# Gates of the spatial layers: the root in halves, pooling by block, and moves issued from two queues

## The chip, the cores and the metric

The program runs on one core of a Trainium2 chip. A core has TensorE (matrix products, written PE; its weight loads PEld), VectorE (DVE), ScalarE (ACT), GpSimd (POOL) and SyncE (SP), each with its own in-order stream of instructions, and 16 DMA engines that move data between and within the memories when an engine issues a transfer. The metric is the device time of one execution in microseconds; less is better. Engines order themselves by semaphores, which the framework places from the reads and writes of tiles.

## The reference

Four layers run on x, eight images of 64 channels and 64 by 64 pixels: a selective scan with a gate behind it, a spatial and channel attention, a modifier with inner gradient steps, and one more attention. The change lies in the gate at the end of the first layer:

```python
def _channel_ln(x, g, b):
    u = jnp.mean(x, 1, keepdims=True)
    v = jnp.mean((x - u) ** 2, 1, keepdims=True)
    return (x - u) * jax.lax.rsqrt(v + CN_EPS) * g[None, :, None, None] + b[None, :, None, None]
...
def _safm(x, mfr_w, mfr_b, aggr_w, aggr_b):
    parts = jnp.split(x, 4, axis=1)
    outs = []
    for i in range(4):
        s = parts[i]
        k = 2 ** i
        if i > 0:
            s = jax.lax.reduce_window(s, -jnp.inf, jax.lax.max, (1, 1, k, k), (1, 1, k, k), 'VALID')
        s = _dwconv3(s, mfr_w[i], mfr_b[i])
        if i > 0:
            s = jnp.repeat(jnp.repeat(s, k, axis=2), k, axis=3)
        outs.append(s)
    out = jnp.concatenate(outs, axis=1)
    out = jnp.einsum('bchw,oc->bohw', out, aggr_w) + aggr_b[None, :, None, None]
    return jax.nn.gelu(out, approximate=False) * x
...
xo = jnp.transpose(xh, (0, 3, 1, 2))
return xo + _safm(_channel_ln(xo, cn_g, cn_b), mfr_w, mfr_b, aggr_w, aggr_b)
```

So each pixel is normalised over its 64 channels; the channels are split into four parts of 16, part i is pooled by maximum over 2^i by 2^i pixels, convolved 3 by 3 channel by channel, brought back to full size, mixed by a 64 by 64 matrix, put through gelu, multiplied with the normalised image, and added to the image.

## The kernel before

`gate_and_attention` works on the images in pairs: the 128 partitions hold 2 images of 64 channels, the free dimension the 4096 pixels. For each of the four pairs (`for p in range(NB // 2)`) it loads x, normalises, gates, and then runs the next layer's attention on it. All of the pair's gate stands on the way to its attention: nothing of another pair lies beside it except the last products of the attention before. "Pair 0" to "pair 3" below are these four.

**Normalisation** (`Common.pair_norm`, L128 to L163). The image is cut into 4 blocks of 1024 pixels (16 image rows). For each block a product with a centring matrix subtracts the mean (L137, tile cps), VectorE copies the result into the interior of the padded image pad0 (L140), ScalarE squares it (L142), and a product with `avg` (L145) puts the variance of 512 pixels into two rows of `var`. One [16, 512] tile thus holds the variance of all pixels. Its root is taken in three steps over 16 partitions: add eps (L150, VectorE), Sqrt (L151, ScalarE), Reciprocal (L152, VectorE). Then for each block a product with `spread`, which has 16 rows, copies the two roots that belong to the block to all channels (L157, tile rps), VectorE multiplies (L162) and ScalarE applies gain and bias (Identity, L163).

**Pooling** (L1473, L1475). When all four blocks are normalised, VectorE takes the maximum over columns and then over rows, for the whole image, three times; the results go to the padded images pad1 (32 by 32), pad2 (16 by 16), pad3 (8 by 8).

**Moves** (`move`, L1423). The convolution is a product over 48 rows per image: 16 channels times three vertical shifts. A tile "mv" holds these, and each is filled by six transfers within SBUF, of 16 partitions each: two images (e) times three shifts (dy). There are tiles for pad3 (1), pad2 (1), pad1 (2) and pad0 (3 tiles for 4 blocks, so that block 3 reuses block 0's), so a pair has 8 moves and 48 transfers. SP issues all of them. Its order in the built program is: three transfers of pad0's first move, both moves of pad1 (12), pad2 (6), pad3 (6), and then the rest of pad0 (21).

**Convolutions** (`conv`, L1433, tile cvps). They run from the smallest image up: pad3, pad2, two of pad1, and four blocks of pad0, each with its result doubled and added to the next (`doubled` L1445, `add_doubled` L1454). A product of 512 columns leaves two records of TensorE in the trace. For each block of pad0 follow gelu on ScalarE (L1504), the product with the normalised image (L1505) and the sum into x (L1506) on POOL.

PSUM comes from three pools: "sc" with three buffers (cps, rps, cvps and the attention's scores), "av" with one (var), and "mm" with one (the attention's small products fps, qps and sumps, and in the setup the transposes tps and bps of the weights). A tile of a pool with one buffer waits until the one before it has been read. The setup of the gate's and the attention's weights (`safm_setup`, `Attention.__init__`; L1060 to L1119 in the trace) is issued ahead of pair 0 and runs beside its normalisation. The framework schedules the instructions of each engine from their order in the program and from when they can run; transfers take eight semaphores in turn, and a transfer waits until the one before it on its semaphore has landed.

Of the kernel before, what the change touches and what calls it, by code (L numbers as in the profile page):

```python
# [10 lines left out]
F32 = mybir.dt.float32  # L11
BF16 = mybir.dt.bfloat16
AF = mybir.ActivationFunctionType
ALU = mybir.AluOpType
# [5 lines left out]
C = 64  # L20
S = 64
L = S * S
BK = 512
NBK = L // BK
# [20 lines left out]
class Common:  # L45
# [60 lines left out]
    def pair_norm_consts(self):  # L106

        nc = self.nc  # L110
        cen = self.tile([2 * C, 2 * C], "p_cen")
        nc.vector.memset(cen, 0.0)
        avg = self.tile([2 * C, 4 * NBK - 2], "p_avg")
        nc.vector.memset(avg, 0.0)
        for e in range(2):
            rows, m = slice(e * C, (e + 1) * C), 2 * NBK - 2 + e
            nc.vector.tensor_scalar(
                cen[rows, rows], self.ident[rows, rows], -1.0 / C, None, ALU.add
            )
            nc.vector.memset(avg[rows, m : m + 1], 1.0 / C)  # L120
        spread = self.tile([2 * NBK, 2 * NBK, C], "p_spread")
        nc.vector.tensor_copy(
            spread,
            self.ident[: 2 * NBK, : 2 * NBK].unsqueeze(2).to_broadcast([2 * NBK, 2 * NBK, C]),
        )
        return cen, avg, spread

    def pair_norm(self, work, sc, var, src, dst, consts, eps, g, b):  # L128

        nc = self.nc
        cen, avg, spread = consts
        for i in range(NBK // 2):
            ps = sc.tile([128, 2, BK], F32, name="cps", tag="sc")
            for e in range(2):
                nc.tensor.matmul(  # L137
                    ps[:, e, :], cen, src[:, bass.ts(2 * i + e, BK)], start=True, stop=True
                )
            nc.vector.tensor_copy(dst(i), ps.rearrange("p e (r c) -> p (e r) c", c=S))  # L140
            sq = work.tile([128, 2, BK], F32, name="sq", tag="blk", bufs=3)
            nc.scalar.activation(sq, ps, AF.Square)  # L142
            for e in range(2):
                m = 2 * (NBK - 1 - 2 * i - e)
                nc.tensor.matmul(  # L145
                    var[: 2 * NBK], avg[:, m : m + 2 * NBK], sq[:, e, :],
                    start=(i + e == 0), stop=(2 * i + e == NBK - 1),
                )
        rstd = work.tile([2 * NBK, BK], F32, name="rstd", tag="rstd", bufs=1)
        nc.vector.tensor_scalar(rstd, var[: 2 * NBK], eps, None, ALU.add)  # L150
        nc.scalar.activation(rstd, rstd, AF.Sqrt)  # L151
        nc.vector.reciprocal(rstd, rstd)  # L152
        for i in range(NBK // 2):
            ps = sc.tile([128, 2, BK], F32, name="rps", tag="sc")
            for e in range(2):
                j = 2 * (2 * i + e)
                nc.tensor.matmul(  # L157
                    ps[:, e, :], spread[:, j : j + 2, :].rearrange("k e c -> k (e c)"), rstd,
                    start=True, stop=True,
                )  # L160
            out = dst(i)
            nc.vector.tensor_tensor(out, out, ps.rearrange("p e (r c) -> p (e r) c", c=S), ALU.mult)  # L162
            nc.scalar.activation(out, out, AF.Identity, bias=b, scale=g)  # L163


class Background:
# [1208 lines left out]
def gate_and_attention(cm, xh, w, a, x1, mixes, x2):  # L1375


    tc, nc = cm.tc, cm.nc
    halves = [slice(e * C, (e + 1) * C) for e in range(2)]
    with ExitStack() as ctx:  # L1380
# [17 lines left out]
        pads = []  # L1398
        for i in range(4):
            n = S // 2**i + 2  # L1400
# [15 lines left out]
        rows = BK // S  # L1416
        q = C // 4

        def move(i, r0, t):

            for e in range(2):
                for dy in range(3):
                    nc.sync.dma_start(  # L1423
                        t[e * C + dy * q : e * C + (dy + 1) * q],
                        pads[i][e * C + i * q : e * C + (i + 1) * q,
                                r0 + dy : r0 + dy + t.shape[1], :],
                    )
# [32 lines left out]
        for p in range(NB // 2):  # L1460
            x = io.tile([2 * C, L], F32, name="x", tag="x")
# [2 lines left out]
            def inner(i):  # L1464
                return pads[0][:, 1 + 2 * i * rows : 1 + 2 * (i + 1) * rows, 1 : S + 1]

            var = avp.tile([128, BK], F32, name="var", tag="av")
            cm.pair_norm(work, sc, var, x, inner, cn, 1e-6, cn_g, cn_b)
            src = pads[0][:, 1 : S + 1, 1 : S + 1]
            for i in range(1, 4):  # L1470
                n = S // 2**i
                m = one.tile([2 * C, 2 * n, n], F32, name=f"max{i}", tag=f"wide{n}")
                nc.vector.tensor_tensor(m, src[:, :, 0::2], src[:, :, 1::2], ALU.max)  # L1473
                src = pads[i][:, 1 : n + 1, 1 : n + 1]
                nc.vector.tensor_tensor(src, m[:, 0::2, :], m[:, 1::2, :], ALU.max)  # L1475
                for r, t in enumerate(moved[i]):
                    move(i, part * r, t)
            p3 = bank(8, 8)
            conv(p3, 3, moved[3][0], 0, 8)
            d3 = doubled(p3, 8, 8)  # L1480
# [33 lines left out]
            for j in range(TQ // 8):  # L1514
                ps = sc.tile([128, 8, 2 * C], F32, name="xTps", tag="sc")
# [674 lines left out]
```

## Time and profile before

Three runs before: median 12229.28 us (12226.62 to 12230.54). The profiled execution took 12228.28 us, its span is 12226.5 us.

| | |
|---|---|
| span of the profiled execution | 12226.5 us |
| busy PE, DVE, ACT, POOL | 11196.6, 10380.4, 7575.7, 7247.3 us |
| the gates: pair 0, from x's issue to x1's issue | 6949.67 to 7060.54 us |
| pair 1, from its first product L137 to x1's issue | 7483.41 to 7577.25 us |
| pair 2 | 7996.81 to 8091.79 us |
| pair 3 | 8514.51 to 8608.30 us |
| transfers of the moves | 192, all issued by SP |

The gates take some 395 us of the span. A row of a timeline gives start, duration, engine, line, operation, result and operands, and in brackets the idle time of the engine ahead of it and what ended it. In stretches, PEclk is the clock that TensorE was granted, as a share of the full one.

### The profile page before, as it was taken

How to read it: one execution, taken by the hardware profiler on the slowest of the kernel's cores; microseconds unless marked ns; L12 is line 12 of the kernel's file. 1: busy time of each engine (PE TensorE's matmuls, PEld its weight loads, DVE VectorE, ACT ScalarE, POOL GpSimd, SP SyncE). 2: the span in 40 equal slices, each digit the busy share in tenths (PEclk: the TensorE clock that was granted, in tenths of full speed). 3: DMA queues.
4: the chain of work that ended last, by engine and by line, in shares of the span. 5: the costliest groups of instructions: out<-in, count | busy, mean ns of one | idle time of the engine just before them, and what ended most of it. 6: DMA issues, size and time to landing. Idle time of an engine off the chain costs nothing. (4 is left out here: it accounts for less than half of the span.)

```text
span 12226.5 us, 120204 instructions
## 1 busy us (share of the span) xinstructions
PE 11196.6 (92%) x39087; PEld 4103.2 (34%) x39087; DVE 10380.4 (85%) x7400; ACT 7575.7 (62%) x10304; POOL 7247.3 (59%) x3326
## 2 busy tenths in 40 slices
PE   7899999999999999999998799999987779999999
PEld 2233333333333333333322233232335463333333
DVE  4999999999999999999999776868778676676767
ACT  4666667766667676676675554645547574555554
POOL 4999999999999999999999500000007480000000
PEclk8999999999999999999999899999998779999999
DMA  3666666666666666666666400000011100000000
GB/s 112 205 210 217 210 211 214 212 212 210 213 212 207 210 216 209 212 213 211 205 203 211 135 20 25 6 25 8 17 49 34 41 20 24 19 4 19 5 11 6
DMA packets 522899, 1528.62 MB, mean 125 GB/s; under 512 B 125312, under 2 KB 142352, under 8 KB 519696
## 3 DMA queue, kind: packets, MB, share of 16 engines
q1 hardware_dynamic: 522256, 1520.80, 37.9%
q8 instruction: 312, 5.11, 0.2%
q14 instruction: 331, 2.71, 0.1%
HBM read 1439.63 MB, written 72.09 MB: 124 GB/s over the span
## 5 line engine op out<-in xcount | busy, mean ns | idle before, releaser
L816 POOL TENSOR_TENSOR ct<-ct,h 128x1024 f32<-128x1024 f32 x2048 | 4789.4, 2362 | 296.8 <-DVE h L811 133.1
L882 PE MATMUL yps<-ct,lno_cen 128*128 128x512 f32 x8192 | 4119.9, 633 | 58.6 <-ACT yps L869 57.2
L811 DVE TENSOR_TENSOR_SCAN h<-a,state,z 128x1024 f32<-128x1024 f32 x1536 | 3570.4, 2341 | 82.5 <-ACT z L777 39.7
L762 ACT ACTIVATE a<-dt,amat 128x1024 f32<-128x1024 f32 x2048 | 2347.1, 1147 | 1134.8 <-DVE h L811 1128.1
L1191 DVE TENSOR_TENSOR sum<-sum,ex 128x1024 f32<-128x1024 f32 x1920 | 2347.5, 1223 | 618.5 <-ACT ex L1184 483.1
L1184 ACT ACTIVATE ex<-sc 128x1024 f32<-128x1024 f32 x2048 | 1968.0, 1024 | 1359.6 <-PE sc L1179 1359.2
L882 PEld LDWEIGHTS yps<-ct,lno_cen 128*128 128x128 f32 x8192 | 1476.4, 195 | 2078.9 <-issue 1818.0
L807 DVE TENSOR_TENSOR z<-z,e 128x1024 f32<-128x1024 f32 x1536 | 1859.8, 1211 | 128.0 <-PE z L780 75.5
L1198 PE MATMUL av<-ex,v 128*64 128x512 f32 x8192 | 1950.0, 604 | 0.0
L1179 PE MATMUL sc<-q,k 16*128 16x512 f32 (+1 forms) x8192 | 1562.1, 623 | 4.2 <-ACT q L1172 3.1
L780 PE MATMUL z<-bs,pick 48*128 48x512 bf16 x3072 | 941.9, 387 | 388.4 <-DVE h L811 339.5
L811 DVE TENSOR_TENSOR_SCAN h<-a,z 128x1024 f32<-128x1024 f32 x512 | 1161.3, 2281 | 75.0 <-ACT z L777 59.8
L770 POOL TENSOR_TENSOR bt<-bt,e 128x1024 f32<-128x1024 f32 x512 | 1209.8, 2363 | 5.4 <-DMA bt<-bc 5.4
L1505 POOL TENSOR_TENSOR gt<-gt,pad 128x1024 f32<-128x1024 f32 x16 | 34.9, 2179 | 1575.0 <-ACT gt L1504 1575.0
L1198 PEld LDWEIGHTS av<-ex,v 128*64 128x64 f32 x8192 | 512.2, 136 | 1332.7 <-issue 1278.9
L1179 PEld LDWEIGHTS sc<-q,k 16*128 16x128 f32 (+1 forms) x8192 | 528.2, 184 | 1016.4 <-issue 977.4
L777 ACT COPY z<-bt 128x1024 f32<-128x1024 f32 x512 | 519.9, 1015 | 406.0 <-DVE h L811 309.2
L780 PEld LDWEIGHTS <-pick 48*128 48x128 bf16 x3072 | 175.9, 95 | 1514.5 <-DVE h L811 931.4
L534 PE MATMUL vps<-pad,convd 128*128 128x512 f32 x1152 | 573.8, 599 | 0.1
L1878 DVE RECIPROCAL r<-e 128x512 f32<-128x512 f32 x128 | 420.6, 3322 | 0.0
L1881 POOL TENSOR_TENSOR r<-r,half 128x512 f32<-128x512 f32 x128 | 162.7, 1271 | 361.9 <-issue 186.0
L798 ACT COPY state<-h 128x1 f32<-128x1 f32 x2048 | 362.9, 177 | 0.0
(417 smaller groups left out, 9594.8 us busy)
## 6 DMA issues: line engine op xcount, KB each, us to landing
ct<-bc SPq DMA_DIRECT2D x2048, 512.0 KB
bt<-bc SPq DMA_DIRECT2D x512, 512.0 KB
x<-x SPq DMA_DIRECT2D x12, 2048.0 KB
bc<-e SPq DMA_DIRECT2D x128, 128.0 KB
x<-x SPq DMA_DIRECT2D x32, 512.0 KB
part<-x SPq DMA_DIRECT2D x128, 128.0 KB
bsd<-bp SPq DMA_DIRECT2D x192, 64.0 KB
bs<-bsd SPq DMA_DIRECT2D x128, 96.0 KB
```

The source lines that it names most:

```text
L534: nc.tensor.matmul(held[0].rearrange("p (r c) -> p r c", c=S), convd[:, t, :], pad[:, j * rows + dy : (j + 1) * rows + dy, dx : dx + S], s ...
L762: ctl["exp", n] = nc.scalar.activation(ctl["a", n], ctl["dt"], AF.Exp, scale=amat[:, ctl["k"], n : n + 1])
L770: nc.gpsimd.tensor_tensor(bt, bt, ctl["dus"], ALU.mult)
L780: nc.tensor.matmul(z[:, bass.ts(i, BK)], pick[:, n : n + 1].to_broadcast([3 * N, DI]), ctl["bs"][:, bass.ts(i, BK)], start=True, stop=True,)
L807: first = nc.vector.tensor_tensor(z, z, ctl["dus"], ALU.mult)
L811: nc.vector.tensor_tensor_scan(h[:, flip], a[:, flip], z[:, flip], 0.0 if state is None else state[:, n : n + 1], ALU.mult, ALU.add,)
L816: freed[at] = nc.gpsimd.tensor_tensor(ct, ct, h, ALU.mult)
L882: nc.tensor.matmul(ctl["ps"][:, bass.ts(i, BK)], lno_cen, ct[:, bass.ts(i, BK)], start=False, stop=(n == N - 1 and not ctl["turns"]),)
L1179: nc.tensor.matmul(sc[:, e, :], k[r : r + d, bass.ts(j, 128)], qs[i][r : r + d, :], start=True, stop=True,)
L1184: nc.scalar.activation(ex, sc, AF.Exp)
L1191: nc.vector.tensor_tensor(sums[i], sums[i], ex, ALU.add)
L1198: nc.tensor.matmul(avs[i][r, :], v[:, j, r], ex[:, e, :], start=(j == 0), stop=(j == TQ - 1))
```

## The change

It changes `pair_norm_consts`, `pair_norm`, `move` and the pair loop of `gate_and_attention`.

- The root is taken in two halves of two blocks each. Each half has its variance in its own PSUM tile (the first in "av" as before, the second, var2, in "mm"); ScalarE's Sqrt reads it with eps as its bias, so that the addition goes; Reciprocal follows for the half. The halves' roots lie at rows 0 to 7 and 32 to 39 of a constant tile p_rstd of 128 rows whose other rows are zero, and spread has 128 rows to match.
- Square comes before the copy in the program.
- A function `ready` is called after each normalised block: it pools the block's rows and starts the moves whose rows are complete. After block 1 pad0's first move, after block 2 pad0's second and pad1's first, after block 3 pad0's third, pad3, pad2 and pad1's second. Only pad0's fourth move stays in the loop of convolutions.
- Of each move the transfers of image e = 0 are issued by SP, those of e = 1 by ScalarE's queue.

In the built program the instructions of the scan, of the attention and of the later layers stand in the same order as before on every engine.

```diff
-        spread = self.tile([2 * NBK, 2 * NBK, C], "p_spread")
-        nc.vector.tensor_copy(
-            spread,
-            self.ident[: 2 * NBK, : 2 * NBK].unsqueeze(2).to_broadcast([2 * NBK, 2 * NBK, C]),
-        )
-        return cen, avg, spread
+        spread = self.tile([128, 2 * NBK, C], "p_spread")
+        for h in range(2):
+            nc.vector.tensor_copy(
+                spread[:, h * NBK : (h + 1) * NBK, :],
+                self.ident[:, 32 * h : 32 * h + NBK].unsqueeze(2).to_broadcast([128, NBK, C]),
+            )
+        rstd = self.tile([128, BK], "p_rstd")
+        nc.vector.memset(rstd, 0.0)
+        eps = self.tile([128, 1], "p_eps")
+        nc.vector.memset(eps, 1e-6)
+        return cen, avg, spread, rstd, eps
...
-            nc.vector.tensor_copy(dst(i), ps.rearrange("p e (r c) -> p (e r) c", c=S))
             sq = work.tile([128, 2, BK], F32, name="sq", tag="blk", bufs=3)
             nc.scalar.activation(sq, ps, AF.Square)
+            nc.vector.tensor_copy(dst(i), ps.rearrange("p e (r c) -> p (e r) c", c=S))
+            h = i // 2
             for e in range(2):
-                m = 2 * (NBK - 1 - 2 * i - e)
+                j = 2 * (i % 2) + e
+                m = 2 * (NBK - 1 - j)
                 nc.tensor.matmul(
-                    var[: 2 * NBK], avg[:, m : m + 2 * NBK], sq[:, e, :],
-                    start=(i + e == 0), stop=(2 * i + e == NBK - 1),
-                )
-        rstd = work.tile([2 * NBK, BK], F32, name="rstd", tag="rstd", bufs=1)
-        nc.vector.tensor_scalar(rstd, var[: 2 * NBK], eps, None, ALU.add)
-        nc.scalar.activation(rstd, rstd, AF.Sqrt)
-        nc.vector.reciprocal(rstd, rstd)
+                    var[h][:NBK], avg[:, m : m + NBK], sq[:, e, :], start=(j == 0), stop=(j == 3)
+                )
+            if i % 2:
+                mine = rstd[32 * h : 32 * h + NBK]
+                nc.scalar.activation(mine, var[h][:NBK], AF.Sqrt, bias=eps[:NBK])
+                nc.vector.reciprocal(mine, mine)
...
             nc.scalar.activation(out, out, AF.Identity, bias=b, scale=g)
+            ready(i)
...
-                    nc.sync.dma_start(
+                    (nc.sync, nc.scalar)[e].dma_start(
...
-            var = avp.tile([128, BK], F32, name="var", tag="av")
-            cm.pair_norm(work, sc, var, x, inner, cn, 1e-6, cn_g, cn_b)
-            src = pads[0][:, 1 : S + 1, 1 : S + 1]
-            for i in range(1, 4):
-                n = S // 2**i
-                m = one.tile([2 * C, 2 * n, n], F32, name=f"max{i}", tag=f"wide{n}")
-                nc.vector.tensor_tensor(m, src[:, :, 0::2], src[:, :, 1::2], ALU.max)
-                src = pads[i][:, 1 : n + 1, 1 : n + 1]
-                nc.vector.tensor_tensor(src, m[:, 0::2, :], m[:, 1::2, :], ALU.max)
-                for r, t in enumerate(moved[i]):
-                    move(i, part * r, t)
+            def ready(b):
+                src = pads[0][:, 1 + 16 * b : 17 + 16 * b, 1 : S + 1]
+                for i in range(1, 4):
+                    n, h = S // 2**i, 16 // 2**i
+                    m = maxima[i - 1][:, 2 * h * b : 2 * h * (b + 1), :]
+                    nc.vector.tensor_tensor(m, src[:, :, 0::2], src[:, :, 1::2], ALU.max)
+                    src = pads[i][:, 1 + h * b : 1 + h * (b + 1), 1 : n + 1]
+                    nc.vector.tensor_tensor(src, m[:, 0::2, :], m[:, 1::2, :], ALU.max)
+                if b:
+                    move(0, part * (b - 1), moved[0][b - 1])
+                if b == 2:
+                    move(1, 0, moved[1][0])
+                if b == 3:
+                    for i, r in ((3, 0), (2, 0), (1, 1)):
+                        move(i, part * r, moved[i][r])
+            var = [
+                avp.tile([128, BK], F32, name="var", tag="av"),
+                psum.tile([128, BK], F32, name="var2", tag="mm"),
+            ]
+            cm.pair_norm(work, sc, var, x, inner, cn, cn_g, cn_b, ready)
...
-                move(0, 2 * j * rows, t)
+                if j == 3:
+                    move(0, 2 * j * rows, t)
```

More of the change, by code (lines that the diff above doesn't have):

```diff
@@ L120, in pair_norm_consts, with pair_norm @@
             nc.vector.memset(avg[rows, m : m + 1], 1.0 / C)
-        spread = self.tile([2 * NBK, 2 * NBK, C], "p_spread")
-        nc.vector.tensor_copy(
-            spread,
-            self.ident[: 2 * NBK, : 2 * NBK].unsqueeze(2).to_broadcast([2 * NBK, 2 * NBK, C]),
-        )
-        return cen, avg, spread
-    def pair_norm(self, work, sc, var, src, dst, consts, eps, g, b):
+        spread = self.tile([128, 2 * NBK, C], "p_spread")
[9 more added lines that the diff above has]
+        return cen, avg, spread, rstd, eps
+    def pair_norm(self, work, sc, var, src, dst, consts, g, b, ready):
         nc = self.nc
-        cen, avg, spread = consts
+        cen, avg, spread, rstd, eps = consts
         for i in range(NBK // 2):
@@ L1465, in inner @@
                 return pads[0][:, 1 + 2 * i * rows : 1 + 2 * (i + 1) * rows, 1 : S + 1]
-            var = avp.tile([128, BK], F32, name="var", tag="av")
-            cm.pair_norm(work, sc, var, x, inner, cn, 1e-6, cn_g, cn_b)
-            src = pads[0][:, 1 : S + 1, 1 : S + 1]
-            for i in range(1, 4):
-                n = S // 2**i
-                m = one.tile([2 * C, 2 * n, n], F32, name=f"max{i}", tag=f"wide{n}")
-                nc.vector.tensor_tensor(m, src[:, :, 0::2], src[:, :, 1::2], ALU.max)
-                src = pads[i][:, 1 : n + 1, 1 : n + 1]
-                nc.vector.tensor_tensor(src, m[:, 0::2, :], m[:, 1::2, :], ALU.max)
-                for r, t in enumerate(moved[i]):
-                    move(i, part * r, t)
+            maxima = [
+                one.tile([2 * C, S // 2**i, S // 2 ** (i + 1)], F32, name=f"max{i}", tag=f"wide{S // 2 ** (i + 1)}")
+                for i in range(3)
+            ]
[17 more added lines that the diff above has]
+                psum.tile([128, BK], F32, name="var2", tag="mm"),
+            ]
+            cm.pair_norm(work, sc, var, x, inner, cn, cn_g, cn_b, ready)
             p3 = bank(8, 8)
```

## The prediction

> **What bounds the kernel now.** The change touches only the gate, one stretch per pair of images, four in the run. I read the page's slices first (the gate lies past 6949 us), then the busy time by stretch for pair 1, the timeline of the same stretch, and the two lines of the moves.
>
> Busy time by stretch, core 0 (span start and end; busy us of each engine with counts; granted TensorE clock; DMA share; GB/s):
>
> ```profile
> core 0: us, PE busy (x) PEld busy (x) DVE busy (x) ACT busy (x) POOL busy (x), PEclk, DMA share, GB/s
> ...
> 7504.00:7518.00 14.00, 13.56 (x16) 4.69 (x15) 4.07 (x4) 3.73 (x3) 0.00 (x0) 0.50 0.20 30
> 7518.00:7540.00 22.00, 0.00 (x0) 0.00 (x1) 5.98 (x7) 1.24 (x1) 0.00 (x0) 0.50 0.11 25
> 7540.00:7578.00 38.00, 37.14 (x135) 21.70 (x136) 10.53 (x12) 6.77 (x6) 18.11 (x8) 0.94 0.21 33
> ```
>
> TensorE does 16 records of the spread at half clock for 14 us, then nothing for 22 us, then convolves. The timeline says what it waited for:
>
> ```profile
> 7503.57 13.99 PE L157 MATMUL rps<-rstd,p_spread 16*128 16x512 f32 x16 [4.90 <-DVE rstd L152]
> ...
> 7518.86 1.24 ACT L163 ACTIVATE pad<-pad,cn_b,cn_g 128x1024 f32<-128x1024 f32 x1 [2.17 <-DVE pad L162]
> 7520.13 2.29 DVE L1473 TENSOR_TENSOR max<-pad 128x2048 f32<-128x2048 f32 x1 [1.31 <-ACT pad L163]
> 7523.71 21.83 SPq L1423 DMA_DIRECT2D mv<-pad  x33
> ...
> 7525.23 0.23 DVE L1475 TENSOR_TENSOR pad<-max 128x64 f32<-128x64 f32 x1
> ...
> 7540.03 5.54 PE L1433 MATMUL cvps<-mv,fw 128*128 128x64 f32 x15 [22.47 <-DMA mv<-pad]
> ```
>
> The instructions of the moves' line, and who waited for them (minimum/median/maximum ns):
>
> ```profile
> L1423 SPq DMA_DIRECT2D mv<-pad x192: 507/587/1440, 6997.6 to 8588.8; - x192
> ...
>   PE cvps L1433: 88.8, 4
> ```
>
> The first convolution (8x8) is fed by the last of 24 issues that SP makes from 7523.71: 12 for pad1, 6 for pad2, 6 for pad3, 0.588 us each and 0.632 from start to start, the last at 7538.19. So the serial issue is the bound, 88.8 us over four pairs. From issue to landing take 1.75 us (16x80, by the convolution that waits), 1.8 (16x288), 2.0 (16x544), 2.45 (16x1056), read off the packets and semaphores.
>
> **The change, part by part, for pair 1** (pairs 2 and 3 look the same). I used the order of the built program and put the rows' durations into it.
>
> *Root.* Square goes before the copy, so it no longer waits behind the previous pair's 3.36 us reciprocal (7483.53 to 7486.89): it starts at 7485.5 instead of 7488.0. TensorE then has the same 16 centring, 16 variance and 2 fps records at 0.43 us; the last variance record ends at 7498.4 (before 7498.68). The 0.68 us addition at L150 goes into the Sqrt's bias. Sqrt 0.63 and Reciprocal 3.34 follow: 7502.5 against 7503.43, **0.9 us gained**, not more, because every spread matmul reads all 128 rows of the root and so waits for both halves. The added first reciprocal (3.34) lies on VectorE from 7492.3 to 7495.6; copies 2 and 3 follow to 7498.1, one microsecond before VectorE is wanted again at 7499.1. Without that cover it costs up to 3.3.
>
> *Spread with 128 rows.* The trace: 16 active rows kept TensorE busy 14 us at a granted 0.50, 0.855 us a record; the 128-row convolution started at 0.50 at 7540.03 and ran at 1.0 from 7544.2. The Trainium skill ("TensorE: Matmul & The Clock Gate", Part 1) says that some 3.4 us of sustained matmuls restore the clock, and names no condition on rows. By that rule the shape is not what kept the old spread cold, and the new one would run as it did: g is then 8.0 and the whole 10 us (rival 3). The rows say that 14 us of 16 rows did not restore it and 4 us of 128 rows did; I take the rows. Two bounds: all 16 records warm, 6.9 us, or all cold, 13.7. The gap before the spread shrinks to 4.1 us; in the trace the clock fell 3.2 to 4.6 us after the last variance record. I take warm for two of pairs 1 to 3 and cold for five records, then warm (9.0 us), for one; all-cold is kept for the range.
>
> *Pooling by block.* 24 small operations in place of 6. Rows of the same sizes: 0.69 (512 elements), 0.43 (256), 0.29 (128), 0.23 (64), about 0.2 below; 2.1 us a block. Of 5.3 us after the last normalised block, 2.5 remain.
>
> *Moves on two queues.* ACT now issues half, in its own order: block 0's Identity, 1 issue, block 1's, 2, block 2's, 6, block 3's, then 13 before the gelus. Block 3's Identity therefore stands behind the third pad1 move, which waits until VectorE has pooled block 2. No row shows an issue on ACT. Bounds: 0.5 (SP's fastest) and 1.44 (SP's slowest); I take SP's 0.632, since semaphore instructions take the same 17 ns on both queues.
>
> With these, warm, in us after 7500: multiplications 4.6, 6.3, 8.2, 10.3; block 2's Identity ends 11.6; pad1 is pooled for block 2 at 15.7; third pad1 move 15.7 to 16.3; block 3's Identity ends **17.6** (before 20.1); its pooling **20.1** (25.5). Then pad3's six moves run three per queue. The semaphore lanes are shared by both queues, and ACT's second waits until an earlier SP one has landed (21.9), so ACT's last issue starts at 22.6 and lands at **24.4**: first convolution at 24.4 instead of 40.03. The pad2 moves make the second convolution wait another 1.4. From there the order is unchanged (convolutions 29.8, gelu, products, transposes), so **14.3 us are gained warm, 12.2 with five cold records** (26.5 for the first convolution).
>
> The last move of pad0 now has one issue ahead of the first gelu and two after it: it lands 6.9 us after block 0's convolution, needed after 10.3; 3.4 us of cover. Products on POOL follow the last convolution by 7.2 us, as before.
>
> *Pair 0 is different.* The second half's variance takes the only buffer of the "mm" pool, which the setup of the weights also uses; in the built order it stands behind all three weight transposes, and the second reciprocal behind the bias products. Timeline of pair 0's setup:
>
> ```profile
> 6995.13 0.47 SPq L79 DMA_DIRECT2D wld<-in_L_conv_wv_dram  x1
> ...
> 7000.85 0.31 PE L86 MATMUL tps<-ident,wld 64*64 64x64 f32 x1 [1.36 <-DVE sa_wk L87]
> ...
> 7001.24 0.22 DVE L87 COPY sa_wv<-tps 64x64 f32<-64x64 f32 x1
> ```
>
> wv lands near 6997.2, its copy ends 6997.7, eight variance records mostly cold take 5.7, Sqrt and Reciprocal 4.1: the spread starts at about 7007.7; before it started at 6982.3, running between the setup's own steps to 6999.5. From there as above: first convolution at 7007.7 + 24.0 = 7031.7 against 7022.06; with the 1.4 us and 1.3 us that its colder convolutions lost before, pair 0 is **9.8 us slower**. Put otherwise, its gain is 12.2 less 22.0.
>
> The larger constants (p_rstd, 128-row spread) lie beside the load of x (issued 6949.67, first matmul 6959.20; VectorE had p_cen at 6956.5): nothing, or 1 to 4 us once if that cover goes. The next x now precedes pair 0's moves on SP, but those begin after 7012.
>
> **Sum.** 2 x 14.3 + 12.2 - 9.8 = 31.0 us. Profiled execution 12228.28 (span 12226.5): 12197.3. The median of the runs is 1.0 higher, so I take **12197**. A difference under 0.2% (24.5 us) can't be told from none; the gain is 0.26%.
>
> **Rivals.** With g the gain of an ordinary pair, the whole is 4g - 22.
> 1. *Issues cost more on ACT* (slower). Place: nine issues ahead of block 3's Identity, six more ahead of the first convolution. At 1.0 us g is 11.0, at 1.44 4.1, at 1.8 -2.3; zero overall at 1.33. At 1.8: 31 us slower, **12259**. For: no row of ACT's issues, outliers of 1.37 and 1.44 on SP. Against: equal semaphore instructions.
> 2. *The second queue brings no issue rate.* The skill ("DMA: Bandwidth & Descriptors", section "Issuing engines are not separate DMA queues") says that issuing from several engines saves only the sequencer's time, usually small beside the transfer. Here the row says the opposite: a 16x80 transfer's packets take 0.16 us, its issue 0.63. If both nonetheless share one rate, g is 6.4 and the whole 3.6: **12225**, no change.
> 3. *The spread stays cold with mostly zero rows*: g is 8.0, whole 10: **12218**, no change.
> 4. *Pair 0 is not held up* and all pairs gain: about 56 us, **12172**. Against it stands the built order.
>
> **How the numbers follow.** Forecast 0.55 (its own range 12184 to 12210), rival 1 0.12, rival 2 0.12, rival 3 0.13, rival 4 0.08. Nine tenths of the forecast's own range lies beyond 24.5 us; with rival 4 faster is 0.58, slower is rival 1's 0.12, the rest 0.30. Range 12180 to 12230: leaves out rival 1 and most of rival 4.
>
> **What would show it.** In pairs 1 to 3 the idle time before the 8x8 convolution falls from 22.5 us to about 14; the spread takes 7 to 9 us with a clock near 1; ACT's issues last 0.6 us; block 3's Identity ends 15 us after the root. In pair 0 the spread starts near 7008. Wrong if ACT's issues exceed 1.3 us, if the spread keeps 0.50, or if pair 0's second root is early.

## The result, and the profile after

The changed kernel takes 12197.45 us (median of 12 runs, 12180.29 to 12205.68), the kernel before in the same comparison 12228.81 (12 runs, 12219.06 to 12237.64). The ratio is 0.9974, with a 95% interval of [0.9966, 0.9982]: 31.4 us faster, by medians.

The profiled execution of the changed kernel has a span of 12178.5 us, 48.0 less than before's 12226.5. That difference must be taken apart before it is used. The x of pair 0 is multiplied first at 6943.1 us where it was 6959.2: 16.1 us come from the layers ahead of the gates, which the change does not touch. (In the eleven kernels profiled here, one execution each, that start lies anywhere between 6939.5 and 6973.3 us, and the profiled execution of the changed kernel, 12180.29 us, is the fastest of its twelve. I take this part for scatter.) Another 6.4 us come from two of the stretches between gates, which took 419.6 us each instead of 422.9 and 422.7; before had 6.8 us at half clock in each of them. Behind the last gate the changed kernel takes 0.6 us more. The gates themselves are what the change is about. I measure a gate from its first centring product (cps) to the end of its last sum on POOL. For pair 0 this begins 9.5 us later than the row of the table of the time before, which starts at x's issue; with that load the gates before take 393.5 us.

| gate, us | pair 0 | pair 1 | pair 2 | pair 3 | all four |
|---|---|---|---|---|---|
| before | 101.3 | 93.8 | 95.0 | 93.8 | 383.9 |
| after | 111.7 | 81.8 | 82.2 | 82.1 | 357.8 |
| gained | -10.4 | 12.0 | 12.8 | 11.7 | 26.1 |

The busy time by stretch for pair 1 of the changed kernel shows what TensorE does in the gate (columns as in the prediction; PEclk is the granted clock):

```profile
core 0: us, PE busy (x) PEld busy (x) DVE busy (x) ACT busy (x) POOL busy (x), PEclk, DMA share, GB/s
7494.00:7500.00 6.00, 5.79 (x7) 2.52 (x8) 1.28 (x2) 0.75 (x1) 0.00 (x0) 0.51 0.00 0
7500.00:7504.00 4.00, 4.00 (x10) 1.52 (x8) 3.25 (x4) 1.83 (x3) 0.00 (x0) 1.00 0.37 68
7504.00:7517.00 13.00, 0.15 (x1) 0.00 (x0) 7.51 (x24) 2.39 (x2) 0.00 (x0) 0.61 0.47 97
```

The spread no longer runs cold (at a granted clock of 0.50) to its end: seven records take the first 6 us at 0.51, the rest run at 1.00. Then TensorE stands idle for 13 us, not 22. The timeline of the same stretch, with some rows of ScalarE and VectorE:

```profile
7494.20 9.94 PE L163 MATMUL rps<-p_rstd,p_spread 128*128 128x512 f32 x16 [4.24 <-DVE p_rstd L158]
...
7504.74 4.60 ACTq L1430 DMA_DIRECT2D mv<-pad  x5
...
7509.39 1.24 ACT L169 ACTIVATE pad<-pad,cn_b,cn_g 128x1024 f32<-128x1024 f32 x1 [4.24 <-DVE pad L1487]
...
7510.66 0.69 DVE L1485 TENSOR_TENSOR max<-pad 128x512 f32<-128x512 f32 x1 [0.85 <-ACT pad L169]
...
7512.66 0.18 DVE L1487 TENSOR_TENSOR pad<-max 128x16 f32<-128x16 f32 x1
7517.11 1.51 PE L1440 MATMUL cvps<-mv,fw 128*128 128x64 f32 x6 [12.97 <-DMA mv<-pad]
...
7519.79 1.62 PE L1440 MATMUL cvps<-mv,fw 128*128 128x256 f32 x3 [1.16 <-DMA mv<-pad]
```

Three waits can be read here. The spread waits 4.24 us for the root. Block 3's Identity waits 4.24 us on ScalarE, and what released it is VectorE's pooling (L1487): not data that the Identity needs, but what the pad1 move queued ahead of it on ScalarE waits for. The last of that queue's five issues ends at 7509.34, and the Identity starts at 7509.39. And the first convolution still waits for a move, 12.97 us instead of 22.47.

The instructions of the moves' line (minimum/median/maximum ns), and who waited for them:

```profile
L1430 SPq DMA_DIRECT2D mv<-pad x96: 507/580/835, 6999.2 to 8538.2; - x96
L1430 ACTq DMA_DIRECT2D mv<-pad x96: 514/524/861, 6999.3 to 8538.9; - x96
...
  PE cvps L1440: 57.1, 8
```

Half of the issues went to ScalarE's queue, and one takes no longer there (median 524 ns) than on SP (580 ns). TensorE's wait for moves fell from 88.8 to 57.1 us over the four pairs, now in eight waits, two a pair.

Pair 0, TensorE's rows of its timeline:

```profile
6981.60 0.28 PE L86 MATMUL tps<-ident,wld 64*64 64x64 f32 x1 [3.48 <-DMA wld<-in_L_conv_wv_dram]
6982.28 6.38 PE L152 MATMUL var<-sq,p_avg 128*8 128x512 f32 x8 [0.40 <-DVE sa_wv L87]
6992.81 9.78 PE L163 MATMUL rps<-p_rstd,p_spread 128*128 128x512 f32 x16 [4.15 <-DVE p_rstd L158]
```

The second half's eight variance records start only behind the transpose of the last weight, wv, which waited for its load. The spread starts 49.7 us after the pair's first product; before it was 23.1.

### The profile page after: what moved, and what is told of

It reads as the page before. It is cut to its first block, busy times and chain, and to the rows that moved or that the text cites. A ratio compares the mean times of both kernels' runs of the same rounds, so it can differ in the third digit from the quotient of the medians.

```text
span 12178.5 us, 120276 instructions
## 1 busy us (share of the span) xinstructions
PE 11159.4 (92%) x39087; PEld 4089.4 (34%) x39087; DVE 10399.7 (85%) x7475; ACT 7580.2 (62%) x10308; POOL 7248.0 (60%) x3326
## 5 line engine op out<-in xcount | busy, mean ns | idle before, releaser
L818 DVE TENSOR_TENSOR_SCAN h<-a,state,z 128x1024 f32<-128x1024 f32 x1536 | 3571.0, 2341 | 82.2 <-ACT z L784 39.1
L1529 POOL TENSOR_TENSOR gt<-gt,pad 128x1024 f32<-128x1024 f32 x16 | 34.8, 2176 | 1542.4 <-ACT gt L1528 1542.4
```

The lines of the kernel that those rows point to most:

```text
L818: nc.vector.tensor_tensor_scan(h[:, flip], a[:, flip], z[:, flip], 0.0 if state is None else state[:, n : n + 1], ALU.mult, ALU.add,)
```

## The experiments

All times below are medians against the kernel before on the same chip. The gates' lengths come from one profiled execution of each kernel; pairs 1 to 3 of one execution differ by 0.1 to 2.2 us, while the whole time carries the scatter of the layers ahead. The intervals of the last six rows overlap: by the whole time these six can't be told apart, and what is said of them rests on the gates.

| kernel | time | before | ratio [95%] | pair 0 | pairs 1 to 3, mean | four gates |
|---|---|---|---|---|---|---|
| after | 12197.45 | 12228.81 | 0.9974 [0.9966, 0.9982] | 111.7 | 82.0 | 357.8 |
| var2_in_sc | 12183.05 | 12228.24 | 0.9967 [0.9955, 0.9979] | 91.2 | 83.5 | 341.5 |
| one_queue | 12223.85 | 12228.24 | 0.9998 [0.9989, 1.0006] | 118.2 | 87.1 | 379.4 |
| rows128_alone | 12214.47 | 12228.24 | 0.9989 [0.9981, 0.9998] | 98.0 | 90.0 | 368.1 |
| whole_root | 12174.43 | 12228.24 | 0.9951 [0.9937, 0.9964] | 93.6 | 81.4 | 337.9 |
| wr_identity_free | 12166.13 | 12225.00 | 0.9953 [0.9940, 0.9967] | 90.4 | 81.2 | 334.1 |
| two_roots_mix | 12145.83 | 12225.00 | 0.9944 [0.9930, 0.9957] | 91.3 | 77.4 | 323.5 |
| warm_both | 12162.28 | 12225.00 | 0.9948 [0.9935, 0.9962] | 91.4 | 78.7 | 327.6 |
| two_mix_free | 12153.57 | 12216.22 | 0.9948 [0.9934, 0.9961] | 91.6 | 75.1 | 316.9 |
| two_mix_warm | 12162.46 | 12216.22 | 0.9958 [0.9945, 0.9972] | 91.0 | 77.4 | 323.1 |

My theory after the result: pairs 1 to 3 gain through three parts (a spread that warms up, issue from two queues, pooling and moves by block), and pair 0 loses through one PSUM buffer. The rivals: the second queue brings no issue rate; the clock depends on the gap and not on the rows; pair 0 is slow because of its weights' loads.

### The buffer of pair 0

```diff
         for i in range(NBK // 2):
+            if i == 2:
+                var.append(sc.tile([128, 2, BK], F32, name="var2", tag="sc")[:, 0, :])
             ps = sc.tile([128, 2, BK], F32, name="cps", tag="sc")
...
-                psum.tile([128, BK], F32, name="var2", tag="mm"),
```

> The changed kernel with one edit: the second half's variance tile is taken from the three-buffer pool sc, behind the second centring tile, and no longer from the one-buffer pool mm that the weights' setup also uses. Lengths are from a pair's first centring product to the end of its last sum on POOL; the changed kernel has 111.8 us for pair 0 and 82 for each of pairs 1 to 3. Theory (the setup's transposes hold pair 0 up through that one buffer): pair 0's spread ends some 40 us after its first product, as in the kernel before, and not after 59.5; pair 0 takes about 92.6 us, pairs 1 to 3 stay at 82; about 19 us less than the changed kernel, 12178. Rival A (it is the weights' own transfers that set pair 0's pace, whatever the buffer): pair 0 stays at 108 to 112, 12197. Rival B (the tile takes a buffer that the centring products need): pairs 1 to 3 become 1 to 3 us longer, 12181 to 12187.

Measured: pair 0 91.2 us. TensorE's rows of its timeline:

```profile
6970.30 1.88 PE L154 MATMUL var<-sq,p_avg 128*8 128x512 f32 x4 [1.17 <-ACT sq L148]
6976.42 4.51 PE L165 MATMUL rps<-p_rstd,p_spread 128*128 128x512 f32 x6 [4.24 <-DVE p_rstd L160]
6983.91 0.34 PE L1086 MATMUL bps<-mb,aggr 64*64 64x1 f32 x4 [2.98 <-DMA mb<-in_L_conv_mfr_b_dram]
6984.18 3.57 PE L165 MATMUL rps<-p_rstd,p_spread 128*128 128x512 f32 x4
```

The variance is no longer behind the transposes: its last records wait for the squares alone, and the spread starts 23.5 us after the pair's first product. The wait for the setup is still there in small (2.98 us for a bias load, in the middle of the spread). So the buffer held pair 0 up, and cost it 20.5 us. Rival A falls. Rival B holds too: the centring products of pairs 1 to 3 now share two buffers, their last variance record ends 18.3 us after the first product instead of 15.5, and these pairs are 1.4 us longer on the mean, although their spread took 8.6 to 8.8 us here and 9.9 to 10.1 in the changed kernel.

### No halves

```diff
-                    var[h][:NBK], avg[:, m : m + NBK], sq[:, e, :], start=(j == 0), stop=(j == 3)
+                    var[: 2 * NBK], avg[:, m : m + 2 * NBK], sq[:, e, :],
+                    start=(i + e == 0), stop=(2 * i + e == NBK - 1),
...
-            if i % 2:
-                mine = rstd[32 * h : 32 * h + NBK]
-                nc.scalar.activation(mine, var[h][:NBK], AF.Sqrt, bias=eps[:NBK])
-                nc.vector.reciprocal(mine, mine)
+        mine = rstd[: 2 * NBK]
+        nc.scalar.activation(mine, var[: 2 * NBK], AF.Sqrt, bias=eps[: 2 * NBK])
+        nc.vector.reciprocal(mine, mine)
```

> The changed kernel without the halves: one variance tile and one root of 16 rows as in the kernel before (eps in the Sqrt's bias and 128-row spread kept), so that no tile of the pool mm is taken. Theory (a spread product reads all 128 rows and so waits for both halves; the halves gain nothing in pairs 1 to 3 and cost pair 0 some 19 us): pairs 1 to 3 stay at 82, pair 0 takes about 92.6; 12178. Rival (the first half's root lies out of the way and would otherwise be late): pairs 1 to 3 become up to 3.3 us longer, 85, and the whole about 12188. If halves were worth more than that, pairs 1 to 3 would pass 86.

Measured: pair 0 93.6, pairs 1 to 3 81.4 on the mean, against 82.0 with halves. Pairs 2 and 3, whose spread took the same time as with halves (9.9 and 10.0 us against 10.1), take 82.0 us against 82.2 and 82.1. Two of TensorE's rows in pair 1, for the comparisons below:

```profile
7512.31 1.51 PE L1437 MATMUL cvps<-mv,fw 128*128 128x64 f32 x6 [12.95 <-DMA mv<-pad]
7515.01 5.32 PE L1437 MATMUL cvps<-mv,fw 128*128 128x256 f32 x11 [1.19 <-DMA mv<-pad]
```

The root's end is where it was, 19.7 us after the first product. As they stand in the change, the halves gain nothing and cost pair 0 18 us.

### One queue

```diff
-                    (nc.sync, nc.scalar)[e].dma_start(
+                    nc.sync.dma_start(
```

> The changed kernel with all moves issued by SP and none by ScalarE; order and pooling as in the change. Theory (the serial issue of 0.63 us a transfer bounds the moves, and a second queue halves it): 28 issues follow block 1's normalisation on one queue, so that the pad3 moves are issued up to 21.0 us where two queues need 15.9, and each of pairs 1 to 3 takes about 5 us more (87 against 82), pair 0 too; in all 20 us slower than the changed kernel, about 12217. The prediction's own figure for a single rate was 7.9 us a pair: 90, 12229. Rival (the queues share one rate, or ScalarE's issues cost it what they save, since block 3's normalisation no longer stands behind them): pairs stay at 82 or get 1 to 4 us shorter, 12180 to 12197.

Measured: 26.4 us slower than the changed kernel by medians, 21.6 by the gates: 6.5 in pair 0, and 4.5, 6.1 and 4.6 in the others. Block 3's Identity does end earlier with one queue (33.4 to 34.8 us after the first product, against 36.2 to 36.4), as the rival said, but the moves behind it come later: the first convolution starts at 46.3 to 47.9 instead of 42.6 to 43.0. In pair 1 it waits 18 us for its move, not 13:

```profile
7536.12 1.51 PE L1440 MATMUL cvps<-mv,fw 128*128 128x64 f32 x6 [17.99 <-DMA mv<-pad]
```

The rival falls. The theory's size was right for pairs 1 to 3; the prediction's own 7.9 us a pair was too much. In pairs 1 and 3 the spread happened to be shorter with one queue (8.5 and 8.7 us against 9.9 and 10.1); in pair 2, where it was nearly the same (9.8 against 10.1), the second queue is worth 6.1 us.

### 128 rows alone

```diff
-        spread = self.tile([2 * NBK, 2 * NBK, C], "p_spread")
+        spread = self.tile([128, 2 * NBK, C], "p_spread")
...
+        rstd = self.tile([128, BK], "p_rstd")
+        nc.vector.memset(rstd, 0.0)
...
-        rstd = work.tile([2 * NBK, BK], F32, name="rstd", tag="rstd", bufs=1)
```

> The kernel before with one edit: the root and the spread constant have 128 rows, the other 112 of them zero; one root, one queue and the order as before. In the kernel before, 16 records of the spread took 14.0 us at a granted clock of 0.50 throughout; in the changed kernel 9.9 to 10.2 us. Theory (the granted clock rises only with active rows): the spread takes 9 to 10 us and its second part shows a clock of 1.0; each of pairs 1 to 3 is 4 us shorter (about 90 against 94), pair 0 some 3; about 15 us less than the kernel before, 12214. Rival (the clock follows the time since the idle gap alone, and the changed kernel's shorter gap of 4.2 us against 4.9 is what brought it back): the spread stays at 14 us, and the time at 12229.

Measured: 13.8 us faster than the kernel before by medians, 15.8 by the gates. Busy time by stretch over pair 1's spread, which starts at 7511.04 behind the same gap of 4.90 us as in the kernel before:

```profile
core 0: us, PE busy (x) PEld busy (x) DVE busy (x) ACT busy (x) POOL busy (x), PEclk, DMA share, GB/s
7511.00:7517.00 6.00, 5.96 (x8) 2.65 (x9) 1.22 (x1) 0.91 (x1) 0.00 (x0) 0.53 0.00 1
7517.00:7521.00 4.00, 3.90 (x10) 1.40 (x8) 2.51 (x3) 2.10 (x3) 0.00 (x0) 1.00 0.24 34
```

With the gap unchanged, 16 rows kept the clock at 0.50 for all 14.0 us, and 128 rows, 112 of them zero, had it back at 1.00 within 6 us. The rows decide, and the rival falls. The spread takes 9.9, 9.6 and 8.7 us in the three pairs.

With this the 12.2 us that an ordinary pair gains can be divided by the means of the table: rows 4.2 (94.2 to 90.0), order, pooling and Square 3.0 (90.0 to 87.1), second queue 5.0 (87.1 to 82.0). The middle part is all in which one_queue differs from rows128_alone, the halves and the eps in the Sqrt too; its members were not separated. Each part also carries the change of the spread, which took 14.0, 9.4, 9.0 and 10.1 us on the mean along this row.

### The Identity behind the move

The changed kernel shows a wait of 4.24 us at block 3's Identity. This edit is made on whole_root, where it is 4.21:

```diff
-                if b == 2:
-                    move(1, 0, moved[1][0])
                 if b == 3:
-                    for i, r in ((3, 0), (2, 0), (1, 1)):
+                    for i, r in ((3, 0), (2, 0), (1, 0), (1, 1)):
```

> The whole-root version with one edit: pad1's first move is issued behind block 3's moves of pad3 and pad2, so that block 3's Identity no longer stands behind it on ScalarE. The whole-root version has pairs 1 to 3 at 80.4 to 82.0 us, block 3's Identity ending 35.1 to 36.3 us after a pair's first product, after an idle wait of some 4 us. Theory (the wait is real, but VectorE's pooling of block 2 is late next): the Identity ends at about 32.4, yet the first convolution is only 1 to 1.7 us earlier, a pair as much shorter, the whole about 12169. Rival A (ScalarE's wait is what sets the first convolution): it comes 3.5 to 4 us earlier, pairs at 78, about 12160. Rival B (pad1's moves, now the last, hold up the convolutions of pad1): pairs the same or 1 to 2 us longer, 12174 to 12182.

Measured: 81.2 us on the mean against 81.4, no gain that this can tell; the means hang on whether the clock was at 0.50 for 3.4 or for 6.8 us around the spread. So I compare pairs with the same spread (pair 1, 8.80 us in both). The Identity ends at 32.0 instead of 35.1, the pooling at 36.4 instead of 37.3, the first convolution at 41.3 instead of 41.55. Of 3 us, 0.3 arrived. Two things took the rest. VectorE still had block 2 to pool, as expected (0.9 left). Then the timeline, from the end of the pooling to ScalarE's second issue:

```profile
7504.80 0.18 DVE L1484 TENSOR_TENSOR pad<-max 128x16 f32<-128x16 f32 x1
7505.00 2.41 SPq L1427 DMA_DIRECT2D mv<-pad  x4
7505.01 2.83 ACTq L1427 DMA_DIRECT2D mv<-pad  x2
```

SP makes four issues in 2.41 us, ScalarE two in 2.83. ScalarE's second waits for the semaphore that SP's second pad3 transfer uses; that landed at 7507.29, and the issue starts at 7507.31. In whole_root ScalarE's second pad3 issue also waits for a landing, but starts 1.7 us after the pooling and not 2.3. So a longer wait for a shared semaphore has taken the place of the wait that was removed. Rival A falls. In pair 1 the convolutions then took 33.6 us instead of 31.6. Two things differ there: a further wait of 0.88 us for pad1's move, which is rival B's, and the clock, which was back at 1.00 only 50.7 us after the first product, in whole_root at 47.6. Pairs whose clock agrees through the convolutions too tell more: pair 2 here takes 79.9 us where pair 1 of whole_root took 80.4 (clock back at 47.6 in both), and pair 3 81.7 where pair 3 took 82.0 (49.8 and 49.6), neither with a wait for pad1's move. The edit is worth 0.2 to 0.5 us a pair; rival B showed in one pair of three.

### Two roots that are really separate

The halves could only pay if the spread of blocks 0 and 1 did not read the second half. So each half gets its own tile; pair 0 takes its second variance from sc, the others from mm, which avoids both costs seen above.

```diff
-        rstd = self.tile([128, BK], "p_rstd")
+        rstd = [self.tile([128, BK], f"p_rstd{h}") for h in range(2)]
...
+            if i == 2 and len(var) == 1:
+                var.append(sc.tile([128, 2, BK], F32, name="var2", tag="sc")[:, 0, :])
...
-                mine = rstd[32 * h : 32 * h + NBK]
+                mine = rstd[h][32 * h : 32 * h + NBK]
...
-                    ps[:, e, :], spread[:, j : j + 2, :].rearrange("k e c -> k (e c)"), rstd,
+                    ps[:, e, :], spread[:, j : j + 2, :].rearrange("k e c -> k (e c)"), rstd[i // 2],
...
+            if p:
+                var.append(psum.tile([128, BK], F32, name="var2", tag="mm"))
```

> The changed kernel with the halves made separate: each half's root in a 128-row tile of its own, so that the spread of blocks 0 and 1 reads the first half alone; pair 0 takes the second variance tile from pool sc, the other pairs from mm as in the change. Theory (the one tile p_rstd made every spread product wait for the second half): the spread starts with the last variance product, at 15.6 us after a pair's first product and not at 19.8; the gap of 4.2 us on TensorE goes, and the first eight records show no clock of 0.5; VectorE does its second reciprocal first, so the first multiplication starts at 19.7 (before some 23.5), the last pooling ends near 33.5 (38.4), pairs 1 to 3 take about 77 us (82), pair 0 about 91 (111.8): about 12160. Rival (what follows the spread has other bounds, the issue of the moves on ScalarE behind block 2's pooling above all): pairs stay at 81 to 82, 12175.

Measured: pairs 1 to 3 77.8, 76.8 and 77.6, pair 0 91.3; ratio to the kernel before 0.9944. TensorE's rows in pair 1:

```profile
7462.29 3.60 PE L155 MATMUL var<-sq,p_avg 128*8 128x512 f32 x8
7465.82 3.70 PE L166 MATMUL rps<-p_rstd,p_spread 128*128 128x512 f32 x8
7470.13 3.67 PE L166 MATMUL rps<-p_rstd,p_spread 128*128 128x512 f32 x8 [0.60 <-DVE p_rstd L161]
7487.96 1.51 PE L1443 MATMUL cvps<-mv,fw 128*128 128x64 f32 x6 [14.16 <-DMA mv<-pad]
7490.64 1.62 PE L1443 MATMUL cvps<-mv,fw 128*128 128x256 f32 x3 [1.17 <-DMA mv<-pad]
```

The first eight records of the spread follow the variance without a gap, the second eight after 0.60 us, and all are warm: 0.46 us a record. The first convolution comes 5.1 to 5.2 us earlier in its pair than in the changed kernel. Not all of this is the earlier start: a pair is 4.0 us shorter than in whole_root, and warm_both below, which only keeps the clock up, is 2.7 us shorter.

The same edit that freed the Identity in whole_root was then made here, where VectorE waits 1.76 us for it:

> The version with two separate roots (pairs 1 to 3 at 76.8 to 77.8 us, first convolution 37.4 to 37.7 us after a pair's first product) with pad1's first move issued behind block 3's moves of pad3 and pad2. In the two-root version VectorE waits 1.8 us for block 3's Identity, which waits 4.6 us on ScalarE. Theory (here the wait reaches VectorE): block 3's pooling ends some 1.8 us earlier and so does the first convolution, unless ScalarE's pad3 issues wait for the landing of SP's on a shared semaphore as they did in the whole-root version with the same edit; pairs at 75.5 to 76, the whole about 12140. Rival (the semaphore's wait takes its place again): the first convolution comes 0 to 0.5 us earlier, pairs at 77, 12145.

Measured: block 3's pooling ends 31.5 us after the first product instead of 33.4, the first convolution starts at 36.4 instead of 37.4 to 37.7, and pairs 1 to 3 take 74.9, 75.1 and 75.3. TensorE's rows in pair 1:

```profile
7493.48 1.51 PE L1443 MATMUL cvps<-mv,fw 128*128 128x64 f32 x6 [12.98 <-DMA mv<-pad]
7495.54 4.77 PE L1443 MATMUL cvps<-mv,fw 128*128 128x256 f32 x9 [0.55 <-DMA mv<-pad]
```

Of 1.9 us at the pooling 1.1 arrived at the first convolution; the shared semaphore took part of it, as ScalarE's second pad3 issue again starts (7490.89) with a landing (7490.87). The pairs gained 2.3 on the mean, more than arrived. The rest lies in the convolutions: the second waits 0.55 us for its move and not 1.17, and the clock was back at 1.00 42.4 to 43.1 us after the first product, in two_roots_mix at 44.2 to 46.5. So the theory holds for the first convolution; how the rest divides was not separated. By its gates (316.9 us against 383.9) it is the best version here; by medians it can't be told from two_roots_mix, since the intervals of the two ratios overlap.

### Keeping TensorE busy

whole_root, with products between the last variance and the spread, and behind the spread, that nothing reads:

```diff
+        filler(4, src[:, :BK].rearrange("p (r c) -> p r c", c=S))
...
+        filler(12, dst(2)[:, : BK // S, :])
...
+            def filler(n, rhs):
+                if p and n:
+                    ps = psum.tile([128, BK], F32, name="fill", tag="mm")
+                    for k in range(n):
+                        nc.tensor.matmul(
+                            ps.rearrange("p (r c) -> p r c", c=S), cn[0], rhs,
+                            start=(k == 0), stop=(k == n - 1),
+                        )
```

> The whole-root version with products added that nothing reads: in pairs 1 to 3, 4 products of 512 columns between the last variance product and the spread, and 12 behind the spread, into the free buffer of pool mm, so that TensorE does not stand idle there. Theory (the idle gaps make the clock fall, and work of 128 rows holds it): no 0.5 in the clock of pairs 1 to 3 between the root and the convolutions, the spread takes 6.9 us against 8.8 to 10.0, the convolutions run warm from the first; a pair gains 2 to 3 us in the spread and up to 2 in the convolutions: about 77.5 against 81.4, the whole 12162. Rival A (the clock falls whatever TensorE does there, at the reload of the root): spread and clock as they were, 12174 or later. Rival B (the moves' arrival and not the clock sets the pace of the convolutions): only the spread's 2 to 3 us are gained, and what that gains is not lost again: about 79, 12167.

Measured: pairs 1 to 3 at 78.7, 78.8 and 78.7. TensorE's rows in pair 1:

```profile
7471.87 3.70 PE L1500 MATMUL fill<-x,p_cen 128*128 128x512 f32 x8
7476.17 7.11 PE L161 MATMUL rps<-p_rstd,p_spread 128*128 128x512 f32 x16 [0.60 <-DVE p_rstd L156]
7484.47 10.61 PE L1500 MATMUL fill<-pad,p_cen 128*128 128x512 f32 x24 [1.20 <-ACT pad L167]
7496.26 0.85 PE L1439 MATMUL cvps<-mv,fw 128*128 128x64 f32 x6 [1.17 <-DMA mv<-pad]
7498.93 13.52 PE L1439 MATMUL cvps<-mv,fw 128*128 128x256 f32 x30 [1.81 <-DMA mv<-pad]
```

The spread takes 7.1 us, so it was the gap that made it cold. The first convolution is warm as well (0.85 us; in whole_root 1.51), but the next one then waits 1.81 us for its move, where in whole_root it waits 1.19: what the clock gives, the wait takes back. From there the clock is at 0.50 for another 3.4 us in warm_both and 3.3 in whole_root. Rival B holds; only the spread's part is gained, and the theory was wrong that work up to the first convolution would keep the later ones warm.

Eleven such products behind the spread were added to two_roots_mix:

> The version with two separate roots, and in pairs 1 to 3 11 products of 512 columns behind the spread that nothing reads, so that TensorE does not stand idle for 14 us before the first convolution. In the two-root version the clock is at 0.50 for 17 to 20 us across that gap, and the convolutions take 32.2 to 33.0 us from first to last; in the whole-root version with such products 31.5 to 32.0, in the kernel before, at whose first convolution all moves of the small images had landed, 29.2 to 30.9. Theory (the first convolutions run cold and the rest of their time is the moves' arrival): no 0.5 at the first convolution, convolutions 31.5 us, pairs at 76.3, the whole about 12142. Rival (arrival alone sets their pace): 32.5 to 33, pairs at 77, 12146.

Measured: 77.8, 76.7 and 77.6 us, within 0.04 of two_roots_mix in each pair. TensorE's two rows of the first convolutions of pair 1:

```profile
7504.62 0.85 PE L1444 MATMUL cvps<-mv,fw 128*128 128x64 f32 x6 [0.80 <-DMA mv<-pad]
7507.31 7.97 PE L1444 MATMUL cvps<-mv,fw 128*128 128x256 f32 x14 [1.84 <-DMA mv<-pad]
```

The second convolution starts 2.69 us after the first, as in two_roots_mix (2.68), whatever the first one took. The number is the rival's. But the clock record has 0.50 again from 7506.55 for 6.8 us, so the later convolutions were no warmer than before, and what warm ones would take stays open. The whole time (12162.46) came out later than that of two_roots_mix, which nothing in the gates explains; the intervals of the two ratios overlap.

## Why the prediction held, step by step

The predicted 12197 us is what was measured. Its mechanism was right, but its sum was 5 us too high: 31.0 by its steps, 26.1 by the gates' lengths, 4.3 of the difference in pairs 1 to 3 and 0.6 in pair 0. That the median still fell on the number is luck. Of the 31.4 us measured, 5.3 lie outside the gates, and over the ten kernels of the table this rest lies anywhere between -7 and 19 us. The last step also has a slip: 31.0 us off the median before, 12229.28, is 12198 and not 12197.

- **The bound.** The first convolution waits for moves that are issued one after the other: right. With one queue the pairs are 5.0 us longer on the mean, so issue does bound them, and a second queue does give issue rate. The section "Issuing engines are not separate DMA queues" of the Trainium skill ("DMA: Bandwidth & Descriptors") calls the sequencer's time usually small beside the transfer. Here it is 0.52 to 0.58 us an issue, where the packets of a 16x80 transfer took 0.16 us in the kernel before, and with many issues in a row it sets the pace. Rival 2 falls.
- **ScalarE's issue.** Taken at SP's 0.632 us from start to start with no row to show it. ScalarE's issues that follow one another without a pause start 0.61 us apart in the median; of 39 such steps all but four lie between 0.55 and 0.65 us, and those four at 0.81 to 0.86. Rival 1, which needed 1.33, falls.
- **The root.** Its end was put at 19.1 us after the pair's first product (7502.5) and came at 19.6. Of the 0.9 us that it was to gain, 0.4 came: the last variance record ends 15.5 us after the first product (15.0 predicted, 15.3 before), so Square ahead of the copy brought nothing there. That the spread waits for both halves was right.
- **The spread.** This is the term that was mis-sized. I took it warm (6.9 us) in two of pairs 1 to 3 and nearly so (9.0) in one. It took 9.94, 10.12 and 10.12, neither the named 7 to 9 us with a clock near 1 nor rival 3's 0.50 to the end. The row of the kernel before was right against the Trainium skill's rule that names no rows ("TensorE: Matmul & The Clock Gate", Part 1), as rows128_alone shows; but in all three pairs the clock fell inside the gap of 4.2 us, 3.1 to 3.5 us after the last variance record, and stayed at 0.50 for 6.8 us, two steps of 3.4 in the trace's clock record. With the prediction's five-record choice, 12.2 us for each of the three, its sum would have been 26.8, against 26.1.
- **Pooling and Identity.** Block 3's Identity ends 36.2 us after the first product (34.2 predicted, the spread's excess), held behind ScalarE's third pad1 move as the prediction said. The pooling follows at 38.4 (36.7).
- **First convolution.** 42.6 to 43.0 us after the first product; 41.0 predicted warm, 43.1 with five cold records. That ScalarE's second pad3 issue waits for a landing on a shared semaphore was foreseen, 1.8 us after the pooling, and it came 1.7 after it. The idle time before the first convolution is 12.97 us; about 14 was named. The second one waits 1.16 (1.4).
- **Pair 0.** Right in mechanism and size: the spread starts 49.7 us after its first product (48.5), the first convolution at 72.6 (72.5), the pair is 10.4 us longer (9.8). var2_in_sc shows that the buffer was the reason. Rival 4 falls.

What the prediction did not see is that the two halves' only measured effect was this loss, and that a root tile for each half would have made them pay.

## What to carry to other kernels

A wait of some microseconds on one engine is worth what remains when the next resource is late: follow the chain past it (here the pooling, then a shared semaphore) before pricing its removal, and compare executions in pairs with the same clock. When work is split so that its first half can run ahead, look at what the reader reads: one tile that holds both halves joins them again, and a tile taken from a pool with one buffer ties the work to whatever else uses that pool. Where the whole time scatters by more than the change is worth, measure the stage itself.

## What the runs showed of the hardware

- Rows brought the clock back even where they held zeros: behind the same gap of 4.90 us, products of 128 rows, 112 of them zero, had it at 1.00 after 3.2 to 5.6 us of the spread (rows128_alone, pairs 1 to 3), and products of 16 rows left it at 0.50 for 14.0 us and beyond (before).
- After an idle gap of 4.2 to 4.9 us in front of the spread the clock was at 0.50 for 2.8 us of the spread or more in every profiled pair 1 to 3; after a gap of 0.60 us, with work of 128 rows before it, the records stayed warm (0.44 to 0.46 us). A long gap is not the only way down: in warm_both 0.85 us of work between gaps of 1.17 and 1.81 us was followed by 3.4 us at 0.50.
- Issuing a small transfer took no longer on ScalarE (median 0.524 us) than on SP (0.580).
- The start of the gates, behind layers that none of the edits touches, lay between 6939.5 and 6973.3 us in the eleven profiled executions, one of each kernel. This spread is of the size of the whole effect of the change.
